# An in-place addition of a bias, 64 times 128x512, moved from VectorE to GpSimd in a two-layer graph kernel

## The chip, the core and the metric

The kernel runs on one core of one Trainium2 chip. The core has TensorE (PE in the profile, its weight loads PEld), VectorE (DVE), ScalarE (ACT), GpSimd (POOL) and SyncE (SP, which here only issues transfers). The metric is device microseconds of one execution, as the median over runs. All data is float32.

## What is computed

The input is x, 16 batches of 1024 nodes with 256 features, and one matrix adj of 1024x1024, of which most entries are zero. Two graph layers follow each other. Cut to what matters:

```
# layer 0, for each batch b
feats = x[b] @ W1.T
f1    = feats @ W2 + b2
coefs = softmax(leaky_relu(f1[:, None] + f1[None, :]) + adj, axis=-1)
h     = coefs @ feats + bias2 + x[b]          # <- bias2 + x[b] is the addition of this document

# layer 1, for each batch b
hidden[u, v] = relu(h[u] @ W1a + h[v] @ W1b + b1)
S            = sigmoid(hidden @ W2 + b2)      # wanted only where adj is not zero
a = (S * adj).T @ h
m = (adj.T @ h) * h
z = beta1 * h + beta2 * (a @ Wa + ba) + beta3 * (m @ Wm + bm)
```

The term `bias2 + x[b]` doesn't depend on the softmax. The kernel adds it into the tile that holds x, in place, some time before the softmax's result is added to the same tile.

## The kernel before

All of it is one program, `edge_layers`, whose order is written out by hand. `Timetable` (L347) is a list of entries, each with a planned time in us; `times.at(t, f)` plans f, `times.matmuls(columns, f)` plans f at the present planned time and moves this time on by what the matmuls are reckoned to take. At the end `run` (L366) issues everything sorted by planned time. So each engine's queue has the order of the planned times, and an instruction that waits holds up all that stands behind it on its engine. A second version of the layers, `dense_layers`, is only run when a check of the inputs asks for it, which doesn't happen here.

The work has these stages:

- The first 40 us or so load the inputs, and ScalarE, TensorE and VectorE make `grown`, the exponentials of adj, transposed.
- Until about 350 us VectorE also makes the lists of the nonzero entries of adj (`keyed` L821, `listed` L834: MAX8 and MATCH_REPLACE8 at L836 and L838), and GpSimd writes them to memory with indirect DMAs (`put`, L842).
- From 0 to about 1340 us the 16 batches pass through layer 0 one after the other, some 65 us each at first, and up to 100 us later on. For batch b+1, in the last third of batch b: `turn` (L942) transposes x on TensorE, `keep_turned` (L950) copies the two halves to `xT`, the second half on VectorE (L955); `features` (L986) multiplies by the weights (L991); `keep_features` (L999) takes f on VectorE (L1004) and the scaled features on ScalarE (L1008, L1016), which frees the PSUM tile for the next `features`; `rows_of_f`, `top_of_f`, `keep_f` and `keep_col` (L961 to L984) make one row and one column of exponentials; `spread` (L1023) makes the weights `eT` on VectorE (L1027); `attend` (L1036) multiplies them with the features (L1041), and `keep_h` (L1049) divides and adds the result to the tile of x (L1055). From then on this tile, `held[b]`, holds h.
- From about 385 to 1960 us the scores of the nonzero entries are made for three groups of batches (5, 5 and 6 of them, `GROUPS` L26), in 135 slots for each group. `fetch` (L1189) has GpSimd gather the rows of 128 entries with indirect DMAs, `gu` once for up to 8 slots (L1193) and `gv` for each slot (L1200), three slots ahead of their use; there are 5 buffers `gv`. `compare` (L1223) takes maximum and minimum of gv and gu on VectorE (two instructions a slot, L1229), `sums` (L1236) adds up along the rows on ScalarE (L1243), and `scatter` (L1207) has GpSimd write the scores to memory with an indirect DMA (L1209). The order of a slot is laid down in `scores` (L1253).
- The rest of layer 1 (`message` L1135, `product` L1154, `end` L1074, `weighed` L1103) runs in between, and after 1340 us alone with the scores. From about 1400 us on `gather` (L1335) multiplies the scores, read back and weighted by adj, with the features.

The addition that is changed is `add_bias` (L957). It is planned in `begin` (L1382), four times for each batch, each time for two of the eight 128x256 pieces of `held[b]`:

```
        if h:
            for i in range(C // 2):
                times.at(end + (1.5 if b else 20.0) + 1.5 * i, lambda i=i: add_bias(b, i))
```

Here `end` is the planned end of the second half of the transposes of x. So the four additions are planned 1.5, 3.0, 4.5 and 6.0 us behind it, in batch 0 20 us later. They must wait for the transposes, which read the same tile, and `keep_h` must wait for them. Nobody else reads what they write.

Of the kernel before, what the change touches and what calls it, by code (L numbers as in the profile page):

```python
# [10 lines left out]
ALU = mybir.AluOpType  # L11
# [3 lines left out]
P = 128  # L15
# [356 lines left out]
def edge_layers(  # L372
# [36 lines left out]
    nc = tc.nc  # L409
    B, N, D = x.shape  # L410
# [37 lines left out]
    def rows(src, name, pool=const):  # L448
        t = pool.tile([P, src.shape[0]], F32, name=name)
        nc.scalar.dma_start(out=t, in_=src.partition_broadcast(P))  # L450
        return t
# [7 lines left out]
    bias2_bc = rows(g0_bias2, "bias2_bc", first)  # L459
# [496 lines left out]

    def add_bias(b, i):  # L957
        x = held[b][:, 2 * i : 2 * i + 2, :]
        nc.vector.tensor_tensor(x, x, bias2_bc.unsqueeze(1).to_broadcast([P, 2, D]), ALU.add)

    def rows_of_f(b):  # L961

# [419 lines left out]
    def begin(b, h):  # L1382
        end = times.matmuls(1024, lambda: turn(b, h))
        times.at(end + 0.3, lambda: keep_turned(b, h))
# [3 lines that stand above are left out]
# [381 lines left out]
```

## Time and profile before

| | us |
|---|---|
| median of 3 runs | 2163.06 |
| lowest and highest of these | 2151.82, 2167.94 |
| the profiled execution's own time | 2155.65 |
| span of its instructions in the profile | 2153.9 |
| VectorE busy with the 64 additions (L959) | 42.6 |
| GpSimd busy with gathers gv, gathers gu, scatters | 475.7, 78.5, 504.1 |

The first two lines of numbers come from runs, the rest from one execution that the profiler recorded. A line of the page's groups has an engine, an operation, output and inputs by the program's names, the shapes and the count, then the busy time in us and the mean duration of one in ns, then the time for which the engine stood idle just before these instructions and what ended it. A line of the chain of waits in order of time has a start, a length, and the engine and line that the end of the program was waiting for in this stretch; the chain is followed back from the last instruction. A line of the timeline has start, length, engine, line, operation, tiles, shapes and count, and in brackets an idle time with what ended it.

GpSimd's records of DMAs are the time in which it writes the descriptors; the transfer comes after.

### The profile page before, as it was taken

How to read it: one execution, taken by the hardware profiler on the slowest of the kernel's cores; microseconds unless marked ns; L12 is line 12 of the kernel's file. 1: busy time of each engine (PE TensorE's matmuls, PEld its weight loads, DVE VectorE, ACT ScalarE, POOL GpSimd, SP SyncE). 2: the span in 40 equal slices, each digit the busy share in tenths (PEclk: the TensorE clock that was granted, in tenths of full speed). 3: DMA queues.
4: the chain of work that ended last, by engine and by line, in shares of the span. 5: the costliest groups of instructions: out<-in, count | busy, mean ns of one | idle time of the engine just before them, and what ended most of it. 6: DMA issues, size and time to landing. Idle time of an engine off the chain costs nothing.

```text
span 2153.9 us, 29186 instructions
## 1 busy us (share of the span) xinstructions
PE 2051.1 (95%) x8566; PEld 1563.9 (73%) x8566; DVE 1597.1 (74%) x2572; ACT 1378.5 (64%) x4842; POOL 1130.6 (52%) x986
## 2 busy tenths in 40 slices
PE   7999999999999999989999899989999999999998
PEld 5887787677776767676788777546676766667887
DVE  6798876586876786768778876577798878885544
ACT  4212222386866777677877777577888878885554
POOL 2121211257666676657777766666777566673000
PEclk9999999999999999999999999999999999999999
DMA  6587777688887888789889989899999999997774
GB/s 212 202 330 272 269 292 276 227 254 291 275 279 245 276 278 265 264 266 291 272 305 297 308 280 341 302 356 414 391 398 373 408 404 387 368 395 277 251 241 134
DMA packets 248009, 644.38 MB, mean 299 GB/s; under 512 B 37154, under 2 KB 137506, under 8 KB 245794
## 3 DMA queue, kind: packets, MB, share of 16 engines
q0 software_dynamic: 82528, 349.79, 46.6%
q1 hardware_dynamic: 129474, 258.44, 32.8%
q10 hardware_dynamic: 35840, 34.22, 4.6%
q8 instruction: 69, 1.13, 0.2%
q14 instruction: 98, 0.80, 0.1%
HBM read 479.56 MB, written 162.92 MB: 298 GB/s over the span
## 4 chain that ended last, share of the span: by engine, by line
PE 58%; DVE 18%; issue 7%; ACT 7%; DMA 7%; POOL 2%; POOLq 0%; another core or an unknown queue 0%; ACTq 0%; SPq 0%; DVEq 0%
PE pv L1041 13%; PE pm L1139 13%; PE pzg L1344 9%; PE pp L1079 8%; DVE gv L1229 6%; DMA gv<-pw_d,idx_v 5%; PE pea L1107 4%; ACT gv L1243 4%; PE pzh L1344 3%; PE pz L1159 3%; PE pf L991 3%; DVE eT L1027 3%; DVE apart L1331 1%; PE ph L1061 1%; ACT apart L1326 1%
## 5 line engine op out<-in xcount | busy, mean ns | idle before, releaser
L1243 ACT ACTIVATE gv<-gv 128x272 f32<-128x272 f32 x2058 | 856.3, 419 | 315.9 <-DVE gv L1229 154.0
L1229 DVE TENSOR_TENSOR gv<-gv,gu 128x680 f32<-128x680 f32 (+1 forms) x810 | 707.1, 906 | 94.4 <-DMA gv<-pw_d,idx_v 86.6
L1200 POOL DMA_INDIRECT gv<-pw_d,idx_v x405 | 475.7, 1175 | 363.5 <-ACT gv L1243 252.3
L1209 POOL DMA_INDIRECT sa_d<-lg,idx_s x405 | 504.1, 1245 | 132.7 <-issue 105.7
L1041 PE MATMUL pv<-feats,eT 128*128 128x257 f32 x2048 | 467.3, 381 | 2.3 <-DVE eT L1027 1.4
L1139 PE MATMUL pm<-adj_sb,xh 128*128 128x512 f32 x1024 | 452.5, 595 | 0.3 <-DVE xh L1055 0.3
L1041 PEld LDWEIGHTS pv<-feats,eT 128*128 128x128 f32 x2048 | 385.3, 191 | 60.6 <-issue 3.1
L1344 PE MATMUL pzg<-ha_g,apart 128*128 128x256 f32 x1536 | 370.7, 384 | 23.8 <-DVE apart L1331 19.1
L1243 ACT ACTIVATION_READ_ACCUMULATOR gv<-gv 128x1 f32 x2058 | 388.7, 189 | 0.0
L1139 PEld LDWEIGHTS pm<-adj_sb,xh 128*128 128x128 f32 x1024 | 194.1, 191 | 220.0 <-issue 216.7
L1344 PEld LDWEIGHTS pzg<-ha_g,apart 128*128 128x128 f32 x1536 | 288.9, 191 | 88.5 <-DVE apart L1331 35.5
L1326 ACT COPY apart<-sat 128x640 f32<-128x640 f32 (+1 forms) x192 | 264.1, 1391 | 89.1 <-PE pzh L1344 57.9
L1079 PE MATMUL pp<-wuv,hT 128*128 128x272 f32 x1024 | 257.6, 402 | 20.1 <-ACT row L979 8.9
L1331 DVE TENSOR_TENSOR apart<-apart,adj_sb 128x640 f32<-128x640 f32 (+1 forms) x192 | 165.7, 865 | 123.3 <-ACT apart L1326 118.6
L1079 PEld LDWEIGHTS pp<-wuv,hT 128*128 128x128 f32 x1024 | 196.3, 194 | 74.8 <-ACT row L979 11.5
L1027 DVE SCALAR_TENSOR_TENSOR eT<-row,col,grown 128x256 f32<-128x256 f32 x512 | 222.6, 477 | 27.8 <-ACT col L984 27.8
L843 POOL DMA_INDIRECT table_d<-rec,at x52 | 57.5, 1105 | 275.3 <-DVE rec L836 170.3
L991 PE MATMUL pf<-w1T,xT 128*128 128x257 f32 x512 | 124.3, 396 | 18.4 <-ACT feats L1016 17.0
L1072 ACT COPY hT<-ph 128x512 f32<-128x512 f32 x96 | 55.1, 575 | 130.5 <-PE ph L1061 109.8
L991 PEld LDWEIGHTS pf<-w1T,xT 128*128 128x128 f32 x512 | 99.5, 198 | 40.2 <-ACT feats L1016 24.4
L1107 PE MATMUL pea<-wa,hT 128*128 128x256 f32 x512 | 122.0, 381 | 0.0
L1159 PE MATMUL pz<-wm,mT 128*128 128x256 f32 x512 | 115.7, 379 | 0.0
(184 smaller groups left out, 1619.0 us busy)
## 6 DMA issues: line engine op xcount, KB each, us to landing
sa_d<-zero SPq DMA_DIRECT2D x128, 512.0 KB
sat<-sa_d SPq DMA_DIRECT2D x128, 320.0 KB
sat<-sa_d SPq DMA_DIRECT2D x64, 384.0 KB
pu_d<-end SPq DMA_DIRECT2D x64, 272.0 KB
pw_d<-end SPq DMA_DIRECT2D x64, 272.0 KB
xh<-in_x_dram SPq DMA_DIRECT2D x16, 1024.0 KB
ha_d<-ea SPq DMA_DIRECT2D x64, 256.0 KB
zb_d<-zb ACTq DMA_DIRECT2D x64, 256.0 KB
```

The costliest lines, as they stand in the source:

```text
L991: nc.tensor.matmul(pf[:, i, : D + 1], lhsT=st["xT"][:, h, c * P : (c + 1) * P], rhs=w1T[:, h, :], start=(h == 0), stop=(h == H - 1),)
L1027: nc.vector.scalar_tensor_tensor(st["eT", b, k][:, j, :], st["row"][:, cols], st["col"][:, j : j + 1], grown[:, j, cols], ALU.max, ALU.mult,)
L1041: nc.tensor.matmul(pv[:, : D + 1], lhsT=eT[:, j, i * P : (i + 1) * P], rhs=st["feats", b][:, j, :], start=(j == 0), stop=(j == C - 1),)
L1079: nc.tensor.matmul(pp[:, k, :R], lhsT=st["hTi", b, i][:, h, k * P : (k + 1) * P], rhs=wuv[:, side, h, :], start=(h == 0), stop=(h == H - 1),)
L1107: nc.tensor.matmul(pp[:, k, :], lhsT=st["hTi", b, i][:, h, k * P : (k + 1) * P], rhs=wa[:, h, :], start=(h == 0), stop=(h == H - 1),)
L1139: nc.tensor.matmul(pm, lhsT=held[b][:, c, h * P : (h + 1) * P], rhs=adj_sb[:, c, span], start=(c == 0), stop=(c == C - 1),)
L1200: nc.gpsimd.indirect_dma_start(out=gv, out_offset=None, in_=pw_d[g], in_offset=bass.IndirectOffsetOnAxis(ap=idx_v[:, t, s : s + 1], axis=0),)
L1209: dma = nc.gpsimd.indirect_dma_start(out=sa_d[g], out_offset=bass.IndirectOffsetOnAxis(ap=idx_s[:, t, s : s + 1], axis=0), in_=lg[:, i, : ...
L1229: nc.vector.tensor_tensor(mv, mv, mu, op)
L1243: nc.scalar.activation(one[:, j, :], one[:, j, :], AF.Copy, accum_out=lg[:, i, j : j + 1])
L1326: nc.scalar.copy(apart.rearrange("p g v -> p v g"), sat)
L1344: nc.tensor.matmul(st["pzg", g, vc][j // 4][:, j % 4, :], lhsT=apart[:, j, :], rhs=ha, start=(c == 0 and j % 2 == 0), stop=(c == C - 1 and ...
```

## The change

One instruction changes its engine. Places, planned times, operands and shapes stay.

```diff
     def add_bias(b, i):
         x = held[b][:, 2 * i : 2 * i + 2, :]
-        nc.vector.tensor_tensor(x, x, bias2_bc.unsqueeze(1).to_broadcast([P, 2, D]), ALU.add)
+        nc.gpsimd.tensor_tensor(x, x, bias2_bc.unsqueeze(1).to_broadcast([P, 2, D]), ALU.add)
```

Since the planned times stay, the additions now stand in GpSimd's queue between the `put`s of the lists (batches 1 to 4) or between the gathers and scatters of the slots (batches 6 to 15); in batches 0 and 5 nothing stands close to them.

## The prediction

> **What bounds the kernel now.** I read the page's first part and its chain first: who is busy, and who sets the end.
>
> ```profile
> PE 2051.1 (95%) x8566; PEld 1563.9 (73%) x8566; DVE 1597.1 (74%) x2572; ACT 1378.5 (64%) x4842; POOL 1130.6 (52%) x986
> PE 58%; DVE 18%; issue 7%; ACT 7%; DMA 7%; POOL 2%; POOLq 0%; another core or an unknown queue 0%; ACTq 0%; SPq 0%; DVEq 0%
> ```
>
> TensorE is busy for 95% of the span and holds 58% of the chain. A VectorE instruction that goes away is worth time only where TensorE stood still for it. Then the changed line, in the view by source line, and the chain in order of time around one batch (b=11):
>
> ```profile
> L959 DVE TENSOR_TENSOR xh<-xh,bias_bc x64: 678/682/752, 39.1 to 1254.8; 128x512 f32<-128x512 f32 x64
> ```
>
> ```profile
> 951.11 1.20 DVE xh L959 x2
> ...
> 953.60 0.68 DVE xh L959
> 954.28 0.78 DVE gv L1229
> 955.06 0.60 DVE xh L959
> 955.66 1.55 DVE gv L1229 x2
> ...
> 957.73 0.16 DVE f L1004
> 957.91 0.21 ACT feats L1008
> 958.15 0.85 ACT feats L1016 x2
> 959.00 0.04 issue
> 959.04 1.23 PE pf L991 x2
> ```
>
> The additions take 0.60 us each when back to back. They stand in VectorE's queue between the copy of xT and f (L1004), f lets ScalarE empty the PSUM tile, and TensorE waits for that (pf). So here they are on the path. Adding up L959 over the whole chain gives 20.3 us, in batches 0, 2, 3, 4, 7, 10, 11, 14 and 15.
>
> Last, GpSimd: its waits and VectorE's, and its plain instructions.
>
> ```profile
> POOL gv L1200 <- ACT gv L1243: 252.3, 134, 14.3
> ```
>
> ```profile
> DVE gv L1229 <- DMA gv<-pw_d,idx_v: 86.6, 46, 12.2
> ```
>
> ```profile
> L657 POOL MEMSET zero<- 128x1024 f32 x1 | 0.9, 948 | 0.0
> L525 POOL TENSOR_SCALAR_AFFINE_SELECT upper<-upper 128x128 f32<-128x128 f32 x1 | 0.3, 293 | 0.1
> L535 POOL MEMSET ones<- 128x128 f32 x1 | 0.2, 202 | 0.0
> ```
>
> GpSimd has spare time (252.3 us in which its gathers wait for a buffer that ScalarE frees), but VectorE already waits 86.6 us for gathers that come late. A delay on GpSimd can thus turn into a wait on VectorE.
>
> **The change part by part.**
>
> *Removed from VectorE.* 64 additions by 0.60 to 0.68 us, 42.6 us in all, 2.4 to 2.7 us a batch. What TensorE can get back is no more than it stood idle behind them. In TensorE's timeline, in the 34 us after the transposes of each x, the idle times ended by ScalarE or VectorE work that queues behind the additions are: batch 0 1.4 us (0.68 and 0.67, for `grown`), batch 2 3.4, 3 and 4 1.1 each, 7 0.4, 10 2.9, 11 4.4, 14 3.2 (its two waits for feats), 15 0.2. The 4.7 in batch 8 do not count: VectorE was idle for 3.28 us just before. The waits for `row` and `end` in batches 12, 13 and 15 (2 to 4 us each) come 20 us later, when VectorE had caught up. Capping each batch at 2.4 gives 1.4+2.4+1.1+1.1+0.4+2.4+2.4+2.4+0.2 = 13.8 us. Bounds: 0, when the next in line (ScalarE's sums) is just as late, and the chain's 20.3. I take 13.8.
>
> *Added on GpSimd.* No row shows an addition there. A memset is 202 ns for 128 elements and 948 for 1024, so 0.83 ns an element and 0.10 us fixed, 0.52 us for 512. An affine_select of 128, which also reads one input, is 91 ns above the memset: 0.36 us for each input of 512. Two inputs make 0.52+2x0.36 = 1.25 us. Bounds are 0.5 (inputs free) and 2.3 us (the longest that a scatter's descriptors take in the timeline around 500 us). I take 1.25, with the 0.3 us gap that GpSimd shows between DMAs 1.5 us: 6 us a batch, 97 us in all, where GpSimd gets back 252 us of waiting.
>
> *Its own waits.* The addition waits for TensorE's transposes and holds up the gathers behind it. GpSimd's place in its queue can be read off, as the gather three slots ahead of the last comparison in front of the addition. In batches 6 to 15 it gets there from 1.4 us before the end of the transposes (batch 6, where the next gather waits for ScalarE until later anyhow) to 8 us after. In batches 1 to 4 the `put`s stand there, with 3 to 5 us of idle between any two, and nobody needs them before 385 us. In batch 0 GpSimd is idle from 16 to 81 us. So nothing for the new wait.
>
> *Who waits for the addition.* `keep_h` of the same batch starts 27 to 42 us after the additions on VectorE did (batch 0: 3 us behind the last one, but there GpSimd can begin 25 us earlier). GpSimd's longest wait for a buffer is 14.3 us, so this cover holds; if it were gone, `keep_h` and with it TensorE would be late by the rest.
>
> *Gathers pushed back.* The gathers behind the additions start up to 3 us (two additions) or 6 us (four) later. From the semaphore events a gather lands 7.2 us (median) after its issue. The slack until the comparison needs it, for the first ones behind the additions: batch 7 4.5 us, 10 3.2 (only two additions ahead), 12 3.9, 13 2.1, 14 3.8, 15 4.2; in batches 6, 8, 9 and 11 5.9 and more. What goes beyond: 1.5+0+2.1+3.9+2.2+1.8 = 11.5 us of new waits on VectorE. Of the 40 additions of batches 6 to 15 18 are on the chain, so I count 45%: 5 us. Bounds 0 and 11.5. GpSimd catches up after 10 to 20 us each time, in its waits for ScalarE. The stretch from 1307 to 1400 us, where its gathers are on the chain themselves, begins 50 us after the last addition.
>
> *VectorE and GpSimd beside each other.* A comparison takes 858 ns (median) whether GpSimd writes descriptors all through it (184 of them) or does nothing (67). That speaks for no price. But GpSimd reads no tile then. In the 10 us after the transposes VectorE spends 40% of the time, in batches 6 to 15, in operations with two inputs in SBUF (L1229, L1027, L1169). Bounds per addition: 0, and 1.25 us if it stops VectorE for its whole length. A hit in 40% of the cases makes 0.5; between that and the row of 858 I take 0.25, 10 us on VectorE, 4.5 of it on the path.
>
> The Trainium skill has a rule on this (SBUF — State Buffer, "Who interferes with whom"): a VectorE instruction with two SBUF inputs and a GpSimd instruction that reads SBUF share one read interface, and whichever comes second is held until the first is through. No run here shows it yet; by the rule the price would be nearer to 0.5 us than to 0.25, and the sum below nearer to 0.
>
> **Sum.** -13.8 + 5 + 4.5 = -4.3 us. The profiled execution took 2155.65 us (span 2153.9), so 2151.4; this execution lay 7.4 below the median of the runs, 2163.06. Against that median I forecast 2159 us: a difference that can't be told from none. A measurement here tells about 1% (21.6 us).
>
> **The rivals.**
>
> *Slower: the additions stop VectorE.* If each of the 40 additions beside comparisons stops VectorE for its 1.25 us, that is 50 us, 22 of it on the path: -13.8+5+22 = +13, 2176 us. It turns the sign from (13.8-5)/18 = 0.5 us per addition on the chain. For it: 40% two-input work just there. Against it: the row of 858 ns, and that in batches 10 and 11 VectorE stands idle for 3 and 7 us in the middle of it. In batches 1 to 4 VectorE's work beside it (MAX8, MATCH_REPLACE8) has one input.
>
> *Slower by much: the addition is dear on GpSimd.* At 2.3 us, the scatter's worst, four additions with their gaps keep GpSimd for 10.4 us. Against the same slacks the gathers come late by 47 us over the ten batches, 21 of it on the path at 45%, all 47 at most; with the gain gone that is 2184 to 2210, 2197 in the middle. Against it: the plain rows of 0.2 to 0.95 us. For it: none of these has two inputs, or stands among DMAs.
>
> *Nothing gained.* VectorE's freed time ends in waits for TensorE or ScalarE and the late gathers remain: 0 to +5, 2163 to 2168 us. For it: ScalarE is busy with sums in the same stretch.
>
> *All of it gained.* The chain's whole 20.3 us, without price: 2143 us. Against it: TensorE's idle times allow only 13.8.
>
> **How the numbers follow.** Forecast 0.42, additions that stop VectorE 0.20, dear additions 0.18, nothing gained 0.12, all gained 0.08. Within 1% (2141 to 2185) lie the forecast, nothing gained, three quarters of the first rival, half of the all-gained case and a small rest of the dear one: 0.42+0.12+0.15+0.04+0.01 = 0.74. Slower by over 1%: 0.05 of the first rival and 0.17 of the dear additions, 0.22. Faster: 0.04. The range goes from the full gain (2143) to the first rival with all its late gathers on the path, -13.8+22+11.5 = +20, and half the spread of the runs (16 us) on top: 2190. The forecast's own range is 2150 to 2170.
>
> **What would show it.** In the changed kernel L959 stands on POOL at about 1.25 us, 64 times; VectorE's busy time is 40 us or so lower; TensorE's waits for feats (17.0 us) fall by 5 to 10; VectorE's wait for gathers (86.6) rises by about 10. Contention would show as comparisons longer than 0.86 us beside an addition. The forecast is wrong if the addition takes over 2 us, if VectorE's waits for gathers rise by 30 us or more, or if POOL appears in the waits of `keep_h` (L1055).

## The result, and the profile after

On one chip, the changed kernel takes 2178.48 us (median of 18 runs, 2164.85 to 2190.88) and the kernel before 2164.20 us (18 runs). The ratio is 1.0057, with a 95% interval of 1.0039 to 1.0076: a little slower, where the prediction has -4.3 us. The profiled execution took 2180.68 us, with a span of 2178.5 us.

The page's first line (engine, busy time, share of the span, instructions) and VectorE's comparisons from the page's groups (busy, mean ns of one, then the idle time before them and what ended it), of the changed kernel; the last line has the comparisons of the kernel before:

```profile
PE 2057.5 (94%) x8566; PEld 1568.8 (72%) x8566; DVE 1600.7 (73%) x2508; ACT 1377.5 (63%) x4842; POOL 1236.5 (57%) x1050
...
L1229 DVE TENSOR_TENSOR gv<-gv,gu 128x680 f32<-128x680 f32 (+1 forms) x810 | 748.6, 959 | 110.6 <-DMA gv<-pw_d,idx_v 103.7
...
L1229 DVE TENSOR_TENSOR gv<-gv,gu 128x680 f32<-128x680 f32 (+1 forms) x810 | 707.1, 906 | 94.4 <-DMA gv<-pw_d,idx_v 86.6
```

VectorE has 64 instructions fewer, worth 42.6 us, and is yet as busy as before (1597.1 us then). The same 810 comparisons now take 748.6 us; in the kernel before they took 707.1 us, 906 ns each. So the time that the additions freed on VectorE came back inside other instructions. The view by source line shows that the additions themselves are not the surprise:

```profile
L959 POOL TENSOR_TENSOR xh<-xh,bias_bc x64: 1256/1294/1355, 16.0 to 1277.8; 128x512 f32<-128x512 f32 x64
```

They take 1.29 us on GpSimd (least, median, most), 1.25 was forecast. Now the waits, of VectorE, TensorE (the kernel before below it) and GpSimd (us in total, how often, the longest):

```profile
DVE gv L1229 <- DMA gv<-pw_d,idx_v: 103.7, 48, 11.9
```

```profile
PE pf L991 <- ACT feats L1016: 28.1, 14, 3.9
...
PE pf L991 <- ACT feats L1016: 17.0, 9, 4.7
```

```profile
POOL gv L1200 <- ACT gv L1243: 205.5, 110, 14.2
```

VectorE waits 17 us more for gathers. TensorE's waits for feats, which the change was to shorten, went up from 17.0 to 28.1 us, because VectorE gets to f (L1004) later than before: in batches 6 to 15 the last f of a batch starts 18.7 us behind the transposes on average, and 17.0 in the kernel before. GpSimd paid for its additions out of its spare time, 252.3 to 205.5 us.

Where the comparisons lose their time is seen in the timeline of one place, VectorE first, then GpSimd (start, length, engine, line, operation, tiles, shapes, count):

```profile
449.12 0.48 DVE L1055 SCALAR_TENSOR_TENSOR xh<-pv,inv,xh 128x256 f32<-128x256 f32 x1
449.53 4.69 DVE L1229 TENSOR_TENSOR gv<-gv,gu 128x680 f32<-128x680 f32 x2
454.14 0.15 DVE L1052 RECIPROCAL inv<-pv 128x1 f32<-128x1 f32 x1
454.33 0.48 DVE L1055 SCALAR_TENSOR_TENSOR xh<-pv,inv,xh 128x256 f32<-128x256 f32 x1
454.74 0.15 DVE L1004 TENSOR_SCALAR f<-pf 128x2 f32<-128x2 f32 x1
454.80 1.64 DVE L1229 TENSOR_TENSOR gv<-gv,gu 128x680 f32<-128x680 f32 x2
```

```profile
448.99 3.72 POOL L959 TENSOR_TENSOR xh<-xh,bias_bc 128x512 f32<-128x512 f32 x3
452.87 1.41 POOL L1200 DMA_INDIRECT gv<-pw_d,idx_v  x1 [0.16 <-issue]
```

A pair of comparisons takes 1.64 us at 454.80 and 4.69 us at 449.53. The first of that pair alone takes 3.92 us. It starts in the middle of the first of three additions and ends just after the third. Behind it f comes late. `keep_h` (L1055), which reads one operand from PSUM and two from SBUF tiles of which one is a column, keeps its 0.48 us. In the whole trace 20 comparisons overlap an addition, all 20 are longer than usual (the median of the others of their shape is 0.86 us), by 41.9 us in all, and none of the other comparisons is. In these 20, 37 additions lie: 1.13 us lost for each, of its 1.29.

By place (the stretches end at the same TensorE instructions in both profiles), batches 0 to 4 take 336.5 us before and 337.4 after, batches 5 to 15 955.8 and 977.3, the rest 841.2 and 844.2. The loss lies where comparisons and additions stand side by side.

### The profile page after: what moved, and what is told of

It is laid out like the page before. It is cut to its first block, busy times and chain, and to the rows that moved or that the text cites. A ratio compares the mean times of both kernels' runs of the same rounds, so it can differ in the third digit from the quotient of the medians.

```text
span 2178.5 us, 29303 instructions
## 1 busy us (share of the span) xinstructions
PE 2057.5 (94%) x8566; PEld 1568.8 (72%) x8566; DVE 1600.7 (73%) x2508; ACT 1377.5 (63%) x4842; POOL 1236.5 (57%) x1050
## 3 DMA queue, kind: packets, MB, share of 16 engines
q8 instruction: 69, 1.13, 0.2%
## 4 chain that ended last, share of the span: by engine, by line
PE 27%; DVE 8%; issue 5%; ACT 4%; DMA 4%; POOL 2%; another core or an unknown queue 0%; POOLq 0%; DVEq 0%; ACTq 0%
PE pzg L1344 9%; PE pm L1139 5%; DVE gv L1229 4%; PE pv L1041 4%; PE pzh L1344 3%; DMA gv<-pw_d,idx_v 3%; ACT gv L1243 2%; PE pp L1079 2%; DVE apart L1331 1%; PE pea L1107 1%; PE pz L1159 1%; ACT apart L1326 1%; POOL sa_d L1209 1%; POOL gv L1200 1%; DVE zg L1367 1%
## 5 line engine op out<-in xcount | busy, mean ns | idle before, releaser
L1229 DVE TENSOR_TENSOR gv<-gv,gu 128x680 f32<-128x680 f32 (+1 forms) x810 | 748.6, 959 | 110.6 <-DMA gv<-pw_d,idx_v 103.7
L1200 POOL DMA_INDIRECT gv<-pw_d,idx_v x405 | 479.6, 1184 | 310.9 <-ACT gv L1243 205.5
L1209 POOL DMA_INDIRECT sa_d<-lg,idx_s x405 | 524.1, 1294 | 130.9 <-issue 107.5
L1331 DVE TENSOR_TENSOR apart<-apart,adj_sb 128x640 f32<-128x640 f32 (+1 forms) x192 | 165.9, 866 | 120.4 <-ACT apart L1326 118.3
L1027 DVE SCALAR_TENSOR_TENSOR eT<-row,col,grown 128x256 f32<-128x256 f32 x512 | 222.9, 478 | 27.8 <-ACT col L984 26.4
L991 PE MATMUL pf<-w1T,xT 128*128 128x257 f32 x512 | 128.6, 406 | 28.9 <-ACT feats L1016 28.1
```

The lines of the kernel that those rows point to most:

```text
L991: nc.tensor.matmul(pf[:, i, : D + 1], lhsT=st["xT"][:, h, c * P : (c + 1) * P], rhs=w1T[:, h, :], start=(h == 0), stop=(h == H - 1),)
L1027: nc.vector.scalar_tensor_tensor(st["eT", b, k][:, j, :], st["row"][:, cols], st["col"][:, j : j + 1], grown[:, j, cols], ALU.max, ALU.mult,)
L1200: nc.gpsimd.indirect_dma_start(out=gv, out_offset=None, in_=pw_d[g], in_offset=bass.IndirectOffsetOnAxis(ap=idx_v[:, t, s : s + 1], axis=0),)
L1209: dma = nc.gpsimd.indirect_dma_start(out=sa_d[g], out_offset=bass.IndirectOffsetOnAxis(ap=idx_s[:, t, s : s + 1], axis=0), in_=lg[:, i, : ...
L1229: nc.vector.tensor_tensor(mv, mv, mu, op)
L1331: nc.vector.tensor_tensor(apart, apart, a.unsqueeze(1).to_broadcast([P, SIZE[g], P]), ALU.mult)
```

## The experiments

Two theories of the loss were set against each other. *Held reading* ("theory of the port" or "theory 1" in the expectations): an addition on GpSimd that reads SBUF stops VectorE's comparisons (rival 1). *Queue time* ("theory of the queue", "theory 2"): the additions take GpSimd's time, so gathers start late and VectorE waits for them (the term of 5 us, sized too small). A third question is whether the removal from VectorE was worth the 13.8 us.

The kernel before takes between 2122 and 2164 us in the sessions of runs. So a run is compared only with the kernel before in its own session, and profiles only within one. The sessions are named P to T, in order; n is the runs of the experiment.

| run | edit | session, before | us (n) | ratio (95%) |
|---|---|---|---|---|
| e1_no_add | additions left out | P 2149.89 | 2142.27 (12) | 0.9951 (0.9928 to 0.9974) |
| e2_memset | before, and memsets on GpSimd | P | 2180.14 (6) | 1.0119 (1.0080 to 1.0159) |
| e3_read | before, and reading additions on GpSimd | P | 2175.61 (6) | 1.0108 (1.0073 to 1.0143) |
| e4_spaced | changed, 5.0 us apart | P | 2150.56 (12) | 1.0004 (0.9981 to 1.0027) |
| e5_five_memsets | memsets in place of additions | Q 2125.02 | 2135.62 (6) | 1.0052 (1.0032 to 1.0072) |
| e6_late | changed, 20 us later | Q | 2181.32 (5) | 1.0282 (1.0261 to 1.0302) |
| e7_accumulate | added by DMA | Q | 2225.39 (5) | 1.0481 (1.0459 to 1.0503) |
| e9_after_again | changed | R 2154.45 | 2171.55 (8) | 1.0062 (1.0033 to 1.0092) |
| e10_five_memsets_again | as e5 | R | 2147.41 (12) | 0.9978 (0.9951 to 1.0005) |
| e11_no_add_again | as e1 | R | 2142.47 (12) | 0.9964 (0.9941 to 0.9986) |
| e12_vector_late | before, additions later | S 2122.07 | 2149.24 (5) | 1.0138 (1.0116 to 1.0159) |
| e13_after_third | changed | S | 2154.62 (4) | 1.0148 (1.0131 to 1.0165) |
| e14_five_memsets_third | as e5 | S | 2136.31 (6) | 1.0060 (1.0046 to 1.0074) |
| e15_no_add_third | as e1 | S | 2120.69 (12) | 0.9988 (0.9976 to 0.9999) |
| e16_after_fourth | changed | T 2164.46 | 2182.78 (11) | 1.0065 (1.0038 to 1.0092) |
| e17_spaced_again | as e4 | T | 2165.90 (11) | 1.0008 (0.9980 to 1.0036) |
| e18_spaced_memsets | as e5, 5.0 us apart | T | 2162.00 (11) | 0.9982 (0.9948 to 1.0016) |

### What the removal alone is worth

```diff
     def add_bias(b, i):
-        x = held[b][:, 2 * i : 2 * i + 2, :]
-        nc.vector.tensor_tensor(x, x, bias2_bc.unsqueeze(1).to_broadcast([P, 2, D]), ALU.add)
+        return
```

The kernel leaves the term bias2 out.

> The kernel before with the 64 additions left out altogether (so the output lacks bias2): what VectorE's freed 42.6 us are worth when GpSimd gets nothing for them. Theory of the port (an addition on GpSimd holds up VectorE's comparisons, 41.9 us in the profile after) and theory of the queue (GpSimd's own time makes the gathers late) both keep the prediction's gain: 10 to 14 us below before, about 2152 us. If it lies within 4 us of before, the removal was worth nothing, and the change lost its 14 us to 12 us of harm rather than to 25.

0.49% faster, some 10.5 us, and no queue or reading is added here. That is, in session P, the ceiling of any change that only takes the additions off VectorE. TensorE's waits for feats are shorter than the 17.0 us of the kernel before (its profile is of another session), as the prediction meant them to be:

```profile
PE pf L990 <- ACT feats L1015: 11.9, 9, 5.4
```

### GpSimd's queue without reading, first try

```diff
         nc.vector.tensor_tensor(x, x, bias2_bc.unsqueeze(1).to_broadcast([P, 2, D]), ALU.add)
+        for _ in range(9):
+            nc.gpsimd.memset(spare, 0.0)          # spare: 128x130
```

> The kernel before, additions kept on VectorE, and at each of the 64 places nine memsets of 128x130 on GpSimd (about 1.3 us together), which write a tile of their own and read nothing. GpSimd's queue is as long as in the changed kernel. Theory of the queue: the gathers come late as after the change and nothing is gained, so 20 to 27 us slower than before, 2184 to 2191. Theory of the port: a write alone does not hold up a comparison, so 0 to 6 us slower, 2164 to 2170, and comparisons stay at a mean of 906 ns.

The nine memsets keep GpSimd for 2.37 us at each place (120.4 us busy and 31.3 us of gaps, by 64) and not for the 1.3 us that were meant, nearly twice an addition, and VectorE keeps its own additions. So 1.19% is the price of a much larger queue time and says little about the change's size. What it does show: no comparison is longer (708.0 us in all), and late gathers are the largest effect, 144.6 us of waits. (TensorE also waits 23.1 us for `row`, against 8.9 in the kernel before.)

```profile
L1232 DVE TENSOR_TENSOR gv<-gv,gu 128x680 f32<-128x680 f32 (+1 forms) x810 | 708.0, 906 | 163.8 <-DMA gv<-pw_d,idx_v 144.6 <-issue 9.5 <-ACT gv L1246 5.3
```

### Reading, with VectorE's additions kept

```diff
         nc.vector.tensor_tensor(x, x, bias2_bc.unsqueeze(1).to_broadcast([P, 2, D]), ALU.add)
+        if b > 5:
+            rows = bias2_bc.unsqueeze(1).to_broadcast([P, 2, D])
+            nc.gpsimd.tensor_tensor(pools["spare"], rows, rows, ALU.add)   # bfloat16 out
```

> The kernel before, additions kept on VectorE, and beside those of batches 6 to 15 an addition of 128x512 on GpSimd that reads bias2 twice and writes a bf16 tile nobody needs (about 1.2 us, 40 times). Theory of the port: the comparisons get longer by 35 to 45 us in all (mean 906 to about 955 ns), with no gain against it: 18 to 28 us slower, 2182 to 2192. Theory of the queue: the same as the run with the memsets, whatever that is, with comparisons at 906 ns.

These 40 additions wait for nobody and nobody waits for them. They take 1.25 us each on average. 24 comparisons are longer, by 22.8 us in all, and VectorE's own additions, which also read two SBUF tiles, are longer as well: 42.6 us before, 55.4 here.

```profile
L959 DVE TENSOR_TENSOR xh<-xh,bias_bc 128x512 f32<-128x512 f32 x64 | 55.4, 883 | 0.0
...
L1232 DVE TENSOR_TENSOR gv<-gv,gu 128x680 f32<-128x680 f32 (+1 forms) x810 | 729.8, 934 | 100.6 <-DMA gv<-pw_d,idx_v 88.9 <-issue 10.3 <-ACT gv L1246 1.1
```

The waits for gathers (88.9 us) are about those of the kernel before (86.6, in another session); TensorE's waits for feats are 36.9 us, up from 17.0. So 1.08% is lost with hardly any late gather. That speaks for held reading.

### The additions spaced out

```diff
-                times.at(end + (1.5 if b else 20.0) + 1.5 * i, lambda i=i: add_bias(b, i))
+                times.at(end + (1.5 if b else 20.0) + 5.0 * i, lambda i=i: add_bias(b, i))
```

> The changed kernel with the four additions of a batch planned 5.0 us apart instead of 1.5, so that no two of them stand next to each other in GpSimd's queue. Theory of the port: a comparison meets one addition at most and is held up by 1.3 us instead of up to 3.9, so the comparisons' surplus falls from 41.9 to 15 to 25 us and the time to 2160 to 2170. Theory of the queue: a gather is late by 1.6 us at a time instead of 6, so the time falls to about the same, but the comparisons' surplus would not matter: VectorE's wait for gathers falls from 103.7 to below 90 us.

All 64 additions are still on GpSimd, and nothing is left of the loss: 1.0004. The comparisons lose 19.4 us in place of 41.9, and the longest takes 2.73 us; hardly any is held by more than one addition. Both theories had foretold a shorter time, but the theory of the queue by shorter waits for gathers, below 90 us. They are 119.8 us, more than the 103.7 of the changed kernel's profile (of another session), so the loss doesn't seem to go by way of them. Timeline of one place, VectorE and GpSimd:

```profile
457.06 2.18 DVE L1229 TENSOR_TENSOR gv<-gv,gu 128x680 f32<-128x680 f32 x1
```

```profile
457.23 1.28 POOL L959 TENSOR_TENSOR xh<-xh,bias_bc 128x512 f32<-128x512 f32 x1
```

One addition of 1.28 us makes a comparison 1.32 us longer. By the records the comparison even started 0.17 us ahead of it.

### The queue time of the additions, without their reading

```diff
-        nc.vector.tensor_tensor(x, x, bias2_bc.unsqueeze(1).to_broadcast([P, 2, D]), ALU.add)
+        for _ in range(5):
+            nc.gpsimd.memset(spare, 0.0)          # spare: 128x130
```

The term bias2 is left out. 67.3 us of memsets with 16.6 us of gaps keep GpSimd for 84 us, as the additions do with 80.5 and 4.2.

> The changed kernel with each addition replaced by five memsets of 128x130 on GpSimd (about 1.3 us together, as long as an addition, by the 0.26 us that one took in the run with nine), which read nothing; the additions themselves are left out, so the output lacks bias2. GpSimd's queue is as full as in the changed kernel, VectorE's as empty, only the reading is gone. Theory of the port: little is left of the harm, 4 to 10 us below before, no comparison longer than 1 us. Theory of the queue: as the changed kernel, 8 to 14 us above before.

0.52% is lost on balance by GpSimd's queue time and the removal together, in a session where the kernel before takes 2125 us. No comparison is longer, and VectorE waits 129.9 us for gathers. Since sessions differ, the same was run beside the changed kernel and the removal, twice (R, then S further down).

### The additions later

```diff
-                times.at(end + (1.5 if b else 20.0) + 1.5 * i, lambda i=i: add_bias(b, i))
+                times.at(end + (21.0 + 3.0 * i if b else 20.0 + 1.5 * i), lambda i=i: add_bias(b, i))
```

> The changed kernel with the additions of batches 1 to 15 planned 21, 24, 27 and 30 us behind the transposes instead of 1.5 to 6, that is behind features and f, while TensorE has the long messages to do and before the batch's own attention needs them. If the harm comes from holding VectorE just where f and feats wait for it, this should be 5 to 10 us faster than before. If any place costs the same, it is like the spaced one, 0 to 3 us from before.

The comparisons are held less (13.0 us), but the kernel is 2.8% slower, which neither expectation had. TensorE's waits, of this kernel:

```profile
PE ph L1061 <- DVE xh L1055: 18.2, 9, 3.6
PE pv L1041 <- DVE eT L1027: 15.7, 23, 2.5
```

In e5 of the same session they are 9.8 and 1.4 us. The cover of 27 to 42 us that the prediction named for `keep_h` isn't used up: in the trace every addition ends at least 14.7 us ahead of the `keep_h` that needs it. What the later place meets is `spread` (L1027), which reads `row` and `grown`, two full SBUF tiles, and a column. Its instructions here, then in e5 (in e5 it is line 1028):

```profile
L1027 DVE SCALAR_TENSOR_TENSOR eT<-row,col,grown 128x256 f32<-128x256 f32 x512 | 273.3, 575 | 27.8 <-ACT col L984 27.8
...
L1028 DVE SCALAR_TENSOR_TENSOR eT<-row,col,grown 128x256 f32<-128x256 f32 x512 | 222.8, 478 | 27.0 <-ACT col L985 26.9
```

29 of the 512 overlap an addition, and all 29 are longer, by 50.6 us in all (the longest takes 3.38 us in place of 0.48). With the comparisons and five `over` (L975) VectorE is held for 68 us, more than in the changed kernel, and right in front of what TensorE needs. Batches 0 to 4, where there are no comparisons, take 358.7 us; in e5 they take 335.9. So this run shows held reading on another instruction, and that the place decides the price.

### The addition done by a DMA

```diff
+        if i == 0:
+            nc.gpsimd.dma_start(out=held[b], in_=<bias2 to all rows>, accum_op=ALU.add)
-        nc.vector.tensor_tensor(x, x, bias2_bc.unsqueeze(1).to_broadcast([P, 2, D]), ALU.add)
```

> No engine adds: one DMA for each batch, issued by GpSimd at the first of the four places, adds bias2 from memory into the tile of x as it writes (accumulating DMA). GpSimd has one instruction instead of four and reads no tile. Theory of the port: near the run without additions, 5 to 10 us faster than before. Against it: 16.8 MB more traffic in stages where the DMA engines are 75 to 90% busy, and descriptors that may take GpSimd longer than a gather's 1.2 us; then it is at or above before.

4.8% slower. GpSimd needs only 1.69 us for the descriptors of each of the 16 transfers, but what follows in its queues waits for them to go through:

```profile
POOL gv L1204 <- DMA xh<-in_L_gnn_bias_dram: 38.1, 5, 9.3
```

VectorE waits 205.6 us for gathers. An addition without any engine's reading is thus dearer here than both others.

### The parts side by side, on two chips

The kernel before (e8), the changed kernel, the memsets and the removal, in session R:

> The kernel before once more, for a profile on the chip on which the next three run, since the kernel before took 2164, 2150 and 2125 us on the chips so far. Both theories: ratio 1.00; the stretch of batches 5 to 15 is read from here.

> The changed kernel once more beside the next two on one chip. Both theories: 0.4 to 0.8% slower than before, as measured at first.

> The additions left out and five memsets on GpSimd in each place, once more, on one chip with the changed kernel. Theory of the queue: within 0.3% of the changed kernel, so the reading costs next to nothing on top of GpSimd's time. Theory of the port, if the first result came from the chip: at least 0.6% faster than the changed kernel.

> The additions left out, nothing in their place, on one chip with the two above. Theory of the queue: 0.4 to 0.7% faster than before, and 0.8 to 1.2% faster than with the memsets. If the difference to the run with memsets is below 0.4%, GpSimd's time is not the main cost.

The single run of the kernel before (e8) gave 2155.55 us beside 2154.45. The removal alone is worth 0.36%; with queue time as well it is 0.22% (0.14 points are lost again); with reading it is 0.62% slower (0.84 points more). The intervals of e10 and e11 overlap, so the 0.14 points can't be told from none; those of e9 and e10 are far apart. The comparisons of e9 and of e10, and TensorE's waits for feats in the same order:

```profile
L1229 DVE TENSOR_TENSOR gv<-gv,gu 128x680 f32<-128x680 f32 (+1 forms) x810 | 753.0, 964 | 119.3 <-DMA gv<-pw_d,idx_v 106.0 <-issue 11.8 <-ACT feats L1008 1.2
```

```profile
L1230 DVE TENSOR_TENSOR gv<-gv,gu 128x680 f32<-128x680 f32 (+1 forms) x810 | 707.5, 908 | 132.1 <-DMA gv<-pw_d,idx_v 118.3 <-issue 9.7 <-ACT feats L1017 1.8
```

```profile
PE pf L991 <- ACT feats L1016: 29.6, 11, 6.4
...
PE pf L992 <- ACT feats L1017: 10.4, 8, 2.6
```

The kernel with the longer waits for gathers (e10) is the faster one. What the held comparisons lengthen is TensorE's wait for feats, by 19.2 us here, and from 4.3 (e14) to 28.8 us (e13) in session S. Session S has the three again, and the additions on VectorE at 25 to 29.5 us:

```diff
-                times.at(end + (1.5 if b else 20.0) + 1.5 * i, lambda i=i: add_bias(b, i))
+                times.at(end + (25.0 if b else 20.0) + 1.5 * i, lambda i=i: add_bias(b, i))
```

> The kernel before with the additions kept on VectorE, those of batches 1 to 15 planned 25 to 29.5 us behind the transposes instead of 1.5 to 6: behind features and f, in front of the batch's own attention. If what the removal is worth (0.4 to 0.5%) comes from f and feats no longer standing behind the additions, most of it is had by this move alone, without GpSimd: 4 to 10 us faster than before. If it comes from VectorE's total time, nothing changes (within 3 us).

> The changed kernel a third time, beside the next two. 0.4 to 0.8% slower than before.

> Additions left out, five memsets on GpSimd in each place, a third time. Theory of the port: 0.6 to 1.0% faster than the changed kernel on the same chip, and at most 0.4% slower than without the memsets. Theory of the queue: within 0.3% of the changed kernel.

> Additions left out, nothing in their place, a third time: 0.3 to 0.6% faster than before. What lies between this and the run with memsets is the price of GpSimd's time alone, what lies between that and the changed kernel the price of the reading.

e12 loses 1.38% with no instruction held, and TensorE waits 19.2 us for `keep_h` (`ph`), as in e6 (8.1 us in e15 of the same session). So a place that late, among `spread` and in front of `keep_h`, is bad on either engine. Of the other three, the stretch of batches 5 to 15 in one profile each, first e15 (removal), then e14 (memsets), then e13 (changed). The columns are the stretch, its length, the busy time of PE, PEld, DVE, ACT, POOL with their instructions, the granted clock, the DMA share and GB/s:

```profile
351.00:1278.30 927.30, 911.42 (x3882) 699.65 (x3880) 688.00 (x1242) 669.64 (x2772) 605.32 (x516) 0.99 0.84 282
```

```profile
347.90:1290.30 942.40, 914.79 (x3882) 700.67 (x3881) 689.16 (x1242) 669.58 (x2774) 662.03 (x733) 0.99 0.83 278
```

```profile
349.00:1312.20 963.20, 921.77 (x3882) 706.76 (x3880) 728.58 (x1241) 670.40 (x2772) 682.89 (x560) 0.98 0.82 272
```

From the first to the second only GpSimd has more to do, and the stretch is 15.1 us longer. From the second to the third VectorE becomes 39.4 us busier with one instruction fewer, and 20.8 us are added. By the runs' ratios the two steps are 0.72 and 0.88 points: 15 and 19 us.

### Spacing beside the changed kernel, and what reading still costs then

e17 is the edit of e4; e18 is that of e5 with the additions' places 5.0 us apart.

> The changed kernel once more, as the yardstick of the next two on their chip. Both theories: 0.5 to 1.5% over the kernel before, comparisons lengthened by 42 to 46 us in all.

> GpSimd's additions 5.0 us apart, on the chip of the changed kernel this time. Theory 1 (shared reading in bursts is the larger part of the loss): comparisons lengthened by 15 to 25 us and not by 42 to 46, and the time 7 to 14 us below the changed kernel's. Theory 2 (GpSimd's queue time is the larger part): the same queue time as in the changed kernel, so a time within 4 us of it, whatever the comparisons show.

> The additions are left out and five memsets stand in each of their places, 5.0 us apart: the queue time of the spaced kernel without its reading. Theory 1: no comparison lengthened, and 7 to 12 us below the spaced kernel with additions (half of the 18 us that the additions 1.5 us apart cost over their memsets). Theory 2: within 4 us of it.

The spaced kernel is 0.57 points below the changed one (12 us by the ratios, 17 by the medians), with the same additions on the same engine. This is what the expectation from held reading called for, and not what that from queue time did; the waits for gathers are 110.5 us in e17 and 103.7 in e16. The last step is not decided: the memsets 5.0 us apart lie 3.9 us below the spaced additions, but the intervals of the two ratios overlap, so 7 to 12 us are neither shown nor excluded. Comparisons of e16, e17 and e18:

```profile
L1229 DVE TENSOR_TENSOR gv<-gv,gu 128x680 f32<-128x680 f32 (+1 forms) x810 | 748.1, 958 | 121.6 <-DMA gv<-pw_d,idx_v 103.7 <-issue 17.6
```

```profile
L1229 DVE TENSOR_TENSOR gv<-gv,gu 128x680 f32<-128x680 f32 (+1 forms) x810 | 730.3, 936 | 129.2 <-DMA gv<-pw_d,idx_v 110.5 <-issue 10.6 <-ACT gv L1243 6.7
```

```profile
L1230 DVE TENSOR_TENSOR gv<-gv,gu 128x680 f32<-128x680 f32 (+1 forms) x810 | 707.6, 908 | 130.6 <-DMA gv<-pw_d,idx_v 114.4 <-ACT gv L1244 7.6 <-issue 5.5
```

TensorE's waits for feats, of e16 and of e17:

```profile
PE pf L991 <- ACT feats L1016: 26.2, 13, 6.2
...
PE pf L991 <- ACT feats L1016: 11.1, 8, 4.0
```

Spaced, 19 additions lie beside 19 comparisons that are held, 22.7 us in all; in the changed kernel of the same session 34 lie beside 18, 40.8 us. So each costs about 1.2 us in both. But the other additions aren't free: eleven of them hold short instructions with two SBUF inputs or, once, one input (`f_most` L1020, `over` L975, one `spread`, one `lg` L1270), 13.7 us in all. VectorE's busy time falls only from 1603.3 to 1599.5 us. What spacing changes is the place: in the changed kernel all of the held time lies ahead of the last f of its batch, for which TensorE waits, in e17 20.9 us lie ahead of it and 15.6 behind. Whether the distance between the additions counts in itself, beside their place, no run here shows.

## Why the prediction was wrong, step by step

The parts, by differences of ratios within a session, against the sum on record:

| step | forecast | session R | session S |
|---|---|---|---|
| removal from VectorE | -13.8 us | -0.36% = -7.8 | -0.12% = -2.5 |
| gathers pushed back | +5 | +0.14% = +3.0 | +0.72% = +15.3 |
| VectorE and GpSimd beside each other | +4.5 | +0.84% = +18.1 | +0.88% = +18.7 |
| sum | -4.3 | +0.62% = +13.4 | +1.48% = +31.4 |

**The step that failed** is "VectorE and GpSimd beside each other". It took 0.25 us for each addition, 10 us on VectorE. The profiles of the changed kernel show 40.8 to 45.8 us of lengthened comparisons, 1.13 to 1.20 us for each addition that lies beside one (37 of them in the first profile), close to the upper bound of 1.25 that the prediction had itself named. Two things were wrong in it. The nearest row was taken to be the comparison of 858 ns beside descriptor writing; but the prediction said in the same paragraph that GpSimd reads no tile then, and a row without the disputed feature is no bound for it. And "a hit in 40% of the cases" took VectorE's share of two-input work as the chance of a hit. (The trace of before has 45% for that share.) In a burst far more are hit: a comparison that meets an addition stays until the burst is through, and 37 of the 40 additions lie beside a comparison; even spaced (e17), 29 of the 40 hold something. The share on the path, 45%, came out close in the changed kernel: 18.1 of 45.8 us is 40%, 18.7 of 43.9 is 43%.

**Rival 1** described this in its numbers: 50 us on VectorE, 22 on the path, 2176 us, against 2178.48 measured; and it named 0.5 us per addition as the point from which the sign turns. It had a chance of 0.20. That its time came out so close is partly luck: in session R its gain is too large by 6 us, its gathers by 2 and its held time on the path by 4, and these nearly cancel. The two theories were told apart by writing without reading (e2, e5, e10, e14, e18: no comparison longer), reading without any dependence (e3: longer), and the same reading at other places (e4, e17: loss gone; e6: `spread` longer, loss larger), with waits for gathers that don't follow the time.

The Trainium skill's rule (SBUF — State Buffer, "Who interferes with whom") that a two-input VectorE instruction and a reading GpSimd instruction contend, and that a GpSimd instruction which only writes does not, agrees with these runs on both points (20 of 20 comparisons longer beside additions, none of 810 beside memsets). By its price as the prediction read it, 0.5 us, the sum stood near 0; the runs show 1.13. The prediction's wording of it, "whichever comes second is held until the first is through", falls short in two ways. The comparison at 449.53 us got no turn between three additions (3.92 us in place of 0.86), and by the records 10 of the 20 held comparisons had started ahead of the first addition that held them, by up to 0.52 us.

**The removal** was oversized: 10.5 us (P), 7.8 (R) and 2.5 (S) in place of 13.8, all inside the bounds of 0 and 20.3. Capping TensorE's idle times at 2.4 us took away VectorE's delay but left the next in line unpriced; that this is the reason is argued and not shown.

**Gathers pushed back** was of the right kind, inside its bounds of 0 and 11.5 us in R (where it can't be told from none) and above them in S. The five memsets, which last as long as the additions, are a control that isn't perfect: the first gather behind an addition takes 1.42 us (median of 18), behind the memsets 0.97, some 8 us of GpSimd's time in all that is counted under reading. The waits for gathers, longer with the memsets (118.3 against 106.0 us in R, 134.1 against 96.8 in S), give no sign that this made the difference.

**Right** were: the addition's own 1.25 us (1.29), and with it that it stays below the 2 us of a dear addition (rival 2); no new wait for the transposes (4.2 us of idle before all 64); no wait of `keep_h` for POOL; GpSimd's spare time as the payer. The signs named for a wrong forecast did partly show: VectorE's waits for gathers rose by 17 us, not by 30, but comparisons grew longer, and VectorE's busy time, which should have fallen by 40 us, rose by 3.6.

**Open:** why the removal is worth 0.5% in one session and 0.1% in another, and the queue time 0.1% or 0.7%. The sums of busy times don't tell, and the profiles of different sessions were not subtracted. Also open is by which rule an instruction is passed over: it is nearly always VectorE's, but in e6 one addition (at 496.86 us) takes 3.76 us, beside four comparisons that keep their 0.85. No kernel tried is faster than the one before while it computes the whole reference; the spaced one is level with it.

## What to carry to other kernels

Before work moves to GpSimd, look at what VectorE runs at that place: if both read SBUF tiles, two on VectorE's side, count nearly the whole length of each GpSimd instruction as lost on VectorE, and the whole of a burst for the one instruction that meets it. Then ask who waits behind that place. If the instructions must be there, try them spaced out or moved: 5.0 us apart took the loss from 0.65% to 0.08% here, with VectorE held for nearly as long but less of it ahead of f, and 20 us later, beside `spread`, raised it to 2.8%. And for a cost that no row shows, choose the row that shares the disputed feature, not the one that stands at the same place.

## What the runs showed of the hardware beyond that

A pause of TensorE costs more than its length. In the records the granted clock drops to half for 3.4 us, sometimes for two or three times that, behind some pauses; in batches 5 to 15 of e13 it does so eight times, each time behind a pause of 2.1 to 4.6 us. In these batches of session S, TensorE's pauses (by the lines above, the length less PE's busy time) are 15.9 us (e15), 27.6 (e14) and 41.4 (e13), and the time lost to the halved clock (its length times what the clock lacks to full speed) is 5.1, 8.5 and 15.4 us. From e15 to e13 both together rise by 35.8 us, and the stretch by 35.9: so over a quarter of what held reading and late gathers cost there is clock, and not pauses.

Every VectorE instruction that is held in these traces has all its inputs in SBUF. `keep_h` (one full operand from PSUM, one from SBUF, and a column) keeps its 0.48 us in all 128 cases. The 13 MAX8 and MATCH_REPLACE8 (L836, L838, one input) that overlap additions in the changed kernel keep their usual length, 1.22 and 1.21 us for 1024 elements. But one input is no safe rule: a small TENSOR_SCALAR of the setup (L557, 128x2) takes 4.30 us in place of 0.16 beside the four additions of batch 0 in e16.

The kernel before differs by 2% from session to session (2122 to 2164 us), more than the effect of the change. P and Q, which have the same chip number in the record, gave 2150 and 2125 us.
